# Attention and deformable-convolution block: input of the first projections loaded in blocks of 32 by 32 and transposed by VectorE

## The chip, the cores and the metric

One core of a Trainium2 chip runs the whole program; seven cores are idle. The metric is the device time of one execution in microseconds (us), lower is better.

The engines are named as in the profile: PE is TensorE's matmul stream and PEld its weight loads, DVE is VectorE, ACT is ScalarE, POOL is GpSimd, SP is SyncE. SP, ACT and POOL issue the DMAs of this kernel; SP issues nearly all.

## The reference, cut to what matters

Four images of 64 by 64 pixels with 256 channels (float32) go through two layers.

```
# layer 0, for each image b, n = 4096 tokens, CQ = 32
q, k, v   = x @ wq + bq, x @ wk + bk, x @ wv + bv     # 256 -> 32, 32, 256
x1        = gamma * softmax(q k^T) v + x
# layer 1
h         = ln(x1)
off, mask = heads(gelu(ln(depthwise3x3(h))))          # 288 offsets and 144 masks per token
s         = sum over 9 points of mask * bilinear sample of (h @ inproj)
x2        = x1 + s @ outproj
out       = x2 + fc2(gelu(fc1(ln(x2))))               # 256 -> 1024 -> 256
```

All matmuls are float32.

## The kernel before, in words

The tokens of an image are cut into 16 parts (`u`) of 256 tokens. The kernel is one software pipeline of 64 slots, one for each part of each image. In a slot PE computes the attention of one part (`e`, the energies, at L719 and `acc`, the weighted sum, at L744), and beside it the first projections of a later part, the layer-1 steps `front`, `plan` and `sample` of earlier parts, and the MLP (`back`) of a still earlier one. The projections of part u of image b+1 run in the slot of part u of image b, so slots 0 to 47 hold one projection each and slots 48 to 63 none. The projections of image 0 have no attention to run beside: they are done one after the other at the start, and `e` of slot 0 comes behind them on PE.

The change touches the function `project`, whose steps are:

- `load` (L611): one DMA of SP brings 256 tokens x 256 channels into `xs`, tokens on partitions. For image 0 `xs` lies in one of eight buffers (tag "ex"), later in a single one.
- `turn` (L619, helper at L316): four PE transposes of 128 x 128 against the identity put the part into PSUM (`pt_x`), channels on partitions. For image 0 this takes a bank of the energies, later one of two banks (tag "m") that nearly all small PE results share.
- `copy` (L622): ACT copies `pt_x` to `xT` in SBUF (three buffers).
- `keys` (L626) makes keys and queries in one PSUM tile `pkq` (two banks in turn for image 0); `key_bias` (L634) adds the biases on ACT: two `kT` pieces (L638) and `qT` (L644, two buffers), and SP writes `qT` to DRAM (`qd`, L645), from where `qs` is read for the attention.
- `values` (L647) makes `pv`; `value_bias` (L656) adds the bias on DVE into `V` for image 0 (L659), or into `vs` (L662), which SP stores for later.

The order on PE, DVE, ACT and POOL is written out by hand: every step has a time in the tables `WHEN` and `LATE`, steps are sorted by slot x 60 + that time and issued in this order, and each engine runs its instructions in order. In "project" the table has load -14.4, turn 19.72, copy 23.24, values 37.05, keys 48.45. SP's order is not written out; the framework's scheduler decides it, so an edit can move DMAs on SP.

Two more things set the order at the start. First, the DMAs of SP and ACT use eight completion counters in turn, in the order in which the scheduler placed them: a DMA is issued only when the DMA that had its counter before has landed. The small weights that ACT loads during image 0 (`loads`, L99: `gamma_s`, `g`, `b`, `inw`, ...) take their turns among SP's. Second, DVE has set-up work in the same stretch: the copies of the offset weights (`om_w`, `om_b`, L154 and L158, each behind a DMA that waits for the copy before) and the number tables (L216), which go back and forth with POOL and wait for POOL's DMAs that write zeros.

Of the kernel before, what the change touches and what calls it, by code (L numbers as in the profile page):

```python
# [8 lines left out]
F32 = mybir.dt.float32  # L9
# [7 lines left out]
def tile_attention_dcnv3_block(  # L17
# [23 lines left out]
    nc = tc.nc  # L41
    B, H, W, C = x.shape
    N = H * W
    P = 128
# [15 lines left out]
    xt_ = x.rearrange("b (t q h2) w c -> b t (h2 w) q c", q=2, h2=2)  # L60
    outs = out.rearrange("b h w c -> (b h w) c")
    out_ = outs.rearrange("(g p) c -> p g c", p=P)

    def tiles_of(v):

        return max(2 * v - 1, 0), 1 if v in (0, UN) else 2
# [9 lines left out]
    p1 = ctx.enter_context(tc.tile_pool(name="p1", bufs=1))  # L76
    main = ctx.enter_context(ExitStack())
    kv = main.enter_context(tc.tile_pool(name="kv", bufs=1))
    p8 = main.enter_context(tc.tile_pool(name="p8", bufs=8))
    win = main.enter_context(tc.tile_pool(name="win", bufs=6))  # L80
    ps_e = main.enter_context(tc.tile_pool(name="ps_e", bufs=1, space=bass.MemoryType.PSUM))
# [40 lines left out]
    for odd in range(2):  # L122
        t = const.tile([P, C // P, 4, CQ], F32, name=f"wkq{odd}")
        v = const.tile([P, 1], F32, name=f"bkq{odd}")
        for r in range(4):
            i = (r // 2 + odd) % 2
# [181 lines left out]
    def rows4(r):  # L308
        return slice(r * CQ, (r + 1) * CQ)

    def transposed(src, name, n=2, pool=None, tag="m"):

        pt = (pool or ps).tile([P, C // P, 256], F32, tag=tag, name=f"pt_{name}")
        for k in range(C // P):
            for i in range(n):
                nc.tensor.transpose(  # L316
                    pt[:, k, i * P : (i + 1) * P], src[:, i, k * P : (k + 1) * P], ident
                )
        return pt
# [283 lines left out]
    def project(b, u):  # L603


        n = f"{b}_{u}"
        first = b == 0
        odd = u % 2
        st = {}

        def load():  # L611
            if first:
                xs = p8.tile([P, 2, C], F32, tag="ex", name=f"xs_{n}")
            else:
                xs = p1.tile([P, 2, C], F32, tag="xs", name=f"xs_{n}")
            st["xs"] = xs
            nc.sync.dma_start(xs, xt_[b, u])

        def turn():  # L619
            st["pt"] = transposed(st["xs"], f"x_{n}", 2, *((ps_e, f"e{odd}") if first else ()))  # L620

        def copy():  # L622
            st["xT"] = p3.tile([P, C // P, 256], F32, tag="cT", name=f"xT_{n}")
            nc.scalar.copy(st["xT"], st["pt"])

        def keys():  # L626
            pool, tag = (ps_e, f"e{2 + odd}") if first else (ps, "m")
            st["pkq"] = pkq = pool.tile([P, 256], F32, tag=tag, name=f"pkq_{n}")
            for k in range(C // P):
                nc.tensor.matmul(  # L630
                    pkq, lhsT=wkq[odd][:, k, :], rhs=st["xT"][:, k, :], start=(k == 0), stop=(k == 1)
                )

        def key_bias():  # L634
            pkq = st["pkq"]
            for i in range(2):
                rows = rows4(2 * odd + i)
                nc.scalar.activation(  # L638
                    kTs[b % 2][u // 2][rows, :], pkq[rows, i * P : (i + 1) * P], AF.Identity,
                    bias=bkq[odd][rows, :],  # L640
                )
            rows = rows4(2 - 2 * odd)
            qT = p2.tile([P, 256], F32, tag="qT", name=f"qT_{n}")
            nc.scalar.activation(qT[rows, :], pkq[rows, :], AF.Identity, bias=bkq[odd][rows, :])  # L644
            nc.sync.dma_start(qd[b * NU + u], qT[rows, :])  # L645

        def values():  # L647
            st["pv"] = pv = ps.tile([P, 2, C], F32, tag="m", name=f"pv_{n}")
            for i in range(2):
                for k in range(C // P):  # L650
                    nc.tensor.matmul(  # L651
                        pv[:, i, :], lhsT=st["xT"][:, k, i * P : (i + 1) * P], rhs=wv_s[:, k, :],
                        start=(k == 0), stop=(k == 1),
                    )

        def value_bias():  # L656
            bias = bv_s.unsqueeze(1).to_broadcast([P, 2, C])
            if first:
                nc.vector.tensor_add(V[u][:, :, :C], st["pv"], bias)  # L659
            else:  # L660
                vs = p1.tile([P, 2, C], F32, tag="xq", name=f"vs_{n}")
                nc.vector.tensor_add(vs, st["pv"], bias)  # L662
                nc.sync.dma_start(vd[u], vs)

        return {
            "load": load, "turn": turn, "copy": copy, "keys": keys, "key_bias": key_bias,
            "values": values, "value_bias": value_bias,
        }

# [702 lines left out]
    def whole(general):  # L1372
# [10 lines left out]
        for b in range(B):  # L1383
            for u in range(NU):
                s = b * NU + u
                if b == 0:
                    put(-1, "first", project(b, u), 3.6 * u - 1.8 + WHEN["attention"]["e0"])
                else:
                    put(s - NU, "project", project(b, u))

                    i = u // 4 * 4 + u % 2 * 2
                    t = max(WHEN["attention"][f"w{j}"] for j in (i, i + 1))
                    steps.append(((NU * b - 1) * T + t + 0.5, len(steps), lambda u=u: value_load(u)))
                att = Attention(b, u, general)
                some = att.steps()
                if general and u == 0:
                    put(s, "general", {"e0": some.pop("e0"), "x0": some.pop("x0")})
                put(s, "attention", some)
                put(s, "tables", {k: lambda f=f: ready(f) for k, f in TABLES.items()})
                put(s + 1, "front", front(att))  # L1400
# [95 lines left out]
```

## Time and profile before

| | us |
|---|---|
| median of 3 runs | 3838.01 (3837.57 to 3839.95) |
| the profiled execution, its own time | 3837.92 |
| span of the profiled execution | 3835.8 |
| PE busy | 3789.8 (99%) |
| DVE busy | 3401.7 (89%) |
| ACT busy | 2199.0 (57%) |
| POOL busy | 312.9 (8%) |
| DMA queue of SP, share of 16 DMA engines | 34.5% |
| granted TensorE clock, mean | 0.997 |

An engine's busy time is the union of its instructions' spans; matmuls overlap in the pipeline, so a mean duration of one instruction is longer than what it adds to PE's stream. What an instruction adds is read from the chain of waits, which goes back from the last instruction to whatever released each piece and so counts every microsecond once. In lists of groups the numbers behind the bar are the total busy time (us), the mean of one instruction (ns), then the engine's idle time just before them (us) and what ended it. In a list of windows each row has the stretch, its length, the busy time of PE, PEld, DVE, ACT and POOL with their counts, the granted TensorE clock, the DMA engines' mean busy share and GB/s.

### The profile page before, as it was taken

How to read it: one execution, taken by the hardware profiler on the slowest of the kernel's cores; microseconds unless marked ns; L12 is line 12 of the kernel's file. 1: busy time of each engine (PE TensorE's matmuls, PEld its weight loads, DVE VectorE, ACT ScalarE, POOL GpSimd, SP SyncE). 2: the span in 40 equal slices, each digit the busy share in tenths (PEclk: the TensorE clock that was granted, in tenths of full speed). 3: DMA queues.
4: the chain of work that ended last, by engine and by line, in shares of the span. 5: the costliest groups of instructions: out<-in, count | busy, mean ns of one | idle time of the engine just before them, and what ended most of it. 6: DMA issues, size and time to landing. Idle time of an engine off the chain costs nothing.

```text
span 3835.8 us, 56185 instructions
## 1 busy us (share of the span) xinstructions
PE 3789.8 (99%) x20466; PEld 3139.2 (82%) x20466; DVE 3401.7 (89%) x6199; ACT 2199.0 (57%) x4261; POOL 312.9 (8%) x444
## 2 busy tenths in 40 slices
PE   8999999999999999999999999999999999999988
PEld 7788888888888888888888888888888888888867
DVE  2599899999998998998998999999999999999995
ACT  4556556565565565565565565655655565555543
POOL 1000000000000000000000000000000000000021
PEclk9999999999999999999999999999999999999999
DMA  5333333334343333333533333333344333333331
GB/s 151 91 102 90 96 96 93 99 90 139 97 112 92 102 92 90 106 92 90 149 99 105 97 92 99 91 95 97 100 127 112 91 86 88 98 84 84 88 93 51
DMA packets 231789, 378.03 MB, mean 99 GB/s; under 512 B 32880, under 2 KB 181936, under 8 KB 231504
## 3 DMA queue, kind: packets, MB, share of 16 engines
q1 hardware_dynamic: 221408, 367.46, 34.5%
q10 hardware_dynamic: 8512, 3.43, 0.4%
q8 instruction: 163, 2.67, 0.3%
q0 software_dynamic: 1584, 3.47, 0.3%
q14 instruction: 122, 1.00, 0.1%
HBM read 251.69 MB, written 122.56 MB: 98 GB/s over the span
## 4 chain that ended last, share of the span: by engine, by line
PE 96%; DVE 3%; DMA 1%; ACT 0%; issue 0%; SPq 0%; ACTq 0%; DVEq 0%
PE acc L744 46%; PE ph L1170 11%; PE pmlp L1187 11%; PE e L719 7%; PE po L885 5%; PE pout L1145 3%; PE pp L801 3%; PE pv L651 3%; PE pkq L630 1%; DVE pw L1064 1%; PE pt_p L316 1%; PE pc L861 1%; PE pt_f L316 1%; PE pt_s L316 1%; PE pt_b L316 1%; PE pt_x L316 1%
## 5 line engine op out<-in xcount | busy, mean ns | idle before, releaser
L744 PE MATMUL acc<-V,ex 128*128 128x257 f32 x8192 | 1900.9, 382 | 0.2
L744 PEld LDWEIGHTS acc<-V,ex 128*128 128x128 f32 x8192 | 1532.0, 190 | 264.5 <-issue 64.8
L1064 DVE TENSOR_TENSOR pw<-win,wn 128x1280 f32<-128x1280 f32 x640 | 933.8, 1486 | 9.5 <-ACT wn L1008 1.9
L1072 DVE TENSOR_TENSOR pw<-pw,pw 128x1280 f32<-128x1280 f32 x492 | 731.9, 1488 | 0.1
L732 ACT ACTIVATE ex<-e 128x512 f32<-128x512 f32 x1024 | 529.3, 602 | 63.0 <-PE e L719 54.2
L1170 PE MATMUL ph<-hT_b,f1w 128*128 128x256 f32 (+1 forms) x2080 | 493.2, 380 | 6.3 <-ACT gT L1178 2.8
L1187 PE MATMUL pmlp<-f2w,gT 128*128 128x256 f32 x2048 | 462.7, 379 | 1.3 <-DVE x1b L1152 1.1
L1170 PEld LDWEIGHTS ph<-hT_b,f1w 128*128 128x128 f32 x2080 | 381.9, 190 | 82.8 <-issue 18.9
L848 DVE SCALAR_TENSOR_TENSOR cv<-hs,dw,cv 128x256 f32<-128x256 f32 (+1 forms) x1076 | 429.9, 467 | 7.9 <-ACT cv L844 1.3
L1187 PEld LDWEIGHTS pmlp<-f2w,gT 128*128 128x128 f32 x2048 | 384.2, 190 | 51.8 <-DVE x1b L1152 1.4
L288 ACT ACTIVATE xn_p<-pc,nm_p,rstd_p 128x256 f32<-128x256 f32 x128 | 65.4, 560 | 554.1 <-DVE nm_p L280 551.2
L1178 ACT ACTIVATE gT<-ph,f1b 128x256 f32<-128x256 f32 (+1 forms) x520 | 236.5, 468 | 254.8 <-PE ph L1170 253.3
L719 PE MATMUL e<-qs,kT 32*128 32x256 f32 x4096 | 296.3, 401 | 0.7 <-ACT ex L732 0.7
L719 PEld LDWEIGHTS e<-qs,kT 32*128 32x128 f32 x4096 | 186.7, 184 | 72.3 <-issue 63.3
L732 ACT ACT_TABLE_LOAD x182 | 233.5, 1283 | 3.0
L274 POOL TENSOR_SCALAR rstd_p<-mv_p 128x2 f32<-128x2 f32 (+1 forms) x65 | 76.1, 1171 | 1703.4 <-DVE mv_p L272 1632.4
L885 PE MATMUL po<-om_w,ge 128*128 128x432 f32 x512 | 196.6, 527 | 0.7 <-ACT ge L878 0.7
L974 DVE TENSOR_TENSOR pr<-hat 128x1296 f32<-128x1296 f32 x128 | 192.7, 1505 | 0.6 <-DVE nm_b L280 0.5
L1178 ACT ACT_TABLE_LOAD x124 | 159.1, 1283 | 2.1
L878 ACT ACTIVATE ge<-pt_p,bd,gd 128x256 f32<-128x256 f32 (+1 forms) x130 | 66.0, 558 | 157.0 <-PE pt_p L316 157.0
L885 PEld LDWEIGHTS po<-om_w,ge 128*128 128x128 f32 x512 | 96.9, 190 | 71.1 <-issue 63.3
L894 DVE TENSOR_TENSOR om<-po,om_b 128x432 f32<-128x432 f32 x128 | 77.3, 605 | 87.3 <-PE po L885 87.3
(219 smaller groups left out, 3883.1 us busy)
## 6 DMA issues: line engine op xcount, KB each, us to landing
win<-xp SPq DMA_DIRECT2D x536, 320.0 KB, 4.1
omd<-om SPq DMA_DIRECT2D x63, 432.0 KB, 2.5
xs<-in_x_dram SPq DMA_DIRECT2D x64, 256.0 KB, 5.4
x<-in_x_dram SPq DMA_DIRECT2D x64, 256.0 KB, 2.7
x1d<-x SPq DMA_DIRECT2D x64, 256.0 KB, 3.2
xp<-xq SPq DMA_DIRECT2D x128, 128.0 KB, 2.4
x1b<-x1d SPq DMA_DIRECT2D x63, 256.0 KB, 2.8
spd<-sp SPq DMA_DIRECT2D x63, 256.0 KB, 2.1
```

The lines of the kernel that those rows point to most:

```text
L316: nc.tensor.transpose(pt[:, k, i * P : (i + 1) * P], src[:, i, k * P : (k + 1) * P], ident)
L719: nc.tensor.matmul(es[r][:, jj, :], lhsT=self.kT[2 * g + jj][rows4(r), :], rhs=self.qs[rows4(r), :], start=True, stop=not self.general,)
L732: nc.scalar.activation(ex, self.es[r], AF.Exp)
L744: nc.tensor.matmul(self.acc[i], lhsT=ex[:, jj, i * P : (i + 1) * P], rhs=V[t // 2][:, t % 2, :], start=(g == 0 and r == 0 and jj == 0), st ...
L848: nc.vector.scalar_tensor_tensor(dst, src, dw[:, k, j : j + 1], dst, ALU.mult, ALU.add)
L885: nc.tensor.matmul(st["po", i], lhsT=st["ge"][:, k, i * P : (i + 1) * P], rhs=om_w[:, k, :], start=(k == 0), stop=(k == 1),)
L974: nc.vector.tensor_mul(pr.rearrange("p a b c d g -> p a b (c d g)"), hat[:, :, i, 1, :].unsqueeze(1).to_broadcast([P, 3, 3, S]), hat[:, :, ...
L1064: nc.vector.tensor_mul(st[r].rearrange("p d (g c) -> p (d g) c", c=GC), src.rearrange("p d (g c) -> p (d g) c", c=GC), wns[v][:, i, r] .re ...
L1072: nc.vector.tensor_add(st[0], st[0], st[r])
L1170: nc.tensor.matmul(ph[:, :m], lhsT=f1w[:, k, c * P : (c + 1) * P], rhs=st["hT"][:, k, :m], start=(k == 0), stop=(k == 1),)
L1178: nc.scalar.activation(st["gT"][:, c, :m], st["ph", c][:, :m], AF.Gelu, bias=f1b[:, c : c + 1])
L1187: nc.tensor.matmul(po, lhsT=st["gT"][:, c, i * P : (i + 1) * P], rhs=f2w[:, c, :], start=(c == 0), stop=(c == NH - 1),)
```

## The change

`load` issues four DMAs in place of one, one for each group of 32 partitions, and reads the input in pieces of 32 channels (128 bytes). Within each block of 32 tokens by 32 channels, tokens are still on partitions, but the blocks already lie where the transposed tile needs them: `xs[32i+p, k, 32j+r]` is token 32j+p, channel 128k+32i+r. DVE's transpose then turns every 32 by 32 block in place, and writes `xT` directly from SBUF to SBUF. `turn` and its PSUM tile are gone, and the copy leaves ACT. The transpose on DVE takes the place of `copy` in the hand-written order; its time in the tables is not changed, and nothing else is.

```diff
+    xs_ = x.rearrange("b h w c -> (b h w) c")
+    def in_blocks(dst, src, t0, n):
+        dst = dst.rearrange("p k (j r) -> p k j r", r=32)
+        for i in range(P // 32):
+            nc.sync.dma_start(
+                dst[32 * i : 32 * (i + 1)],
+                bass.AP(
+                    src.tensor, src.offset + t0 * C + 32 * i, [[C, 32], [P, C // P], [32 * C, 4 * n], [1, 32]]
+                ),
+            )
...
             if first:
-                xs = p8.tile([P, 2, C], F32, tag="ex", name=f"xs_{n}")
+                xs = p8.tile([P, C // P, 256], F32, tag="ex", name=f"xs_{n}")
             else:
-                xs = p1.tile([P, 2, C], F32, tag="xs", name=f"xs_{n}")
+                xs = p1.tile([P, C // P, 256], F32, tag="xs", name=f"xs_{n}")
             st["xs"] = xs
-            nc.sync.dma_start(xs, xt_[b, u])
-
-        def turn():
-            st["pt"] = transposed(st["xs"], f"x_{n}", 2, *((ps_e, f"e{odd}") if first else ()))
+            in_blocks(xs, xs_, b * N + 256 * u, 2)
 
         def copy():
             st["xT"] = p3.tile([P, C // P, 256], F32, tag="cT", name=f"xT_{n}")
-            nc.scalar.copy(st["xT"], st["pt"])
+            nc.vector.transpose(st["xT"].rearrange("p k t -> p (k t)"), st["xs"].rearrange("p k t -> p (k t)"))
```

One part's load is 256 pieces of 1 KB before, and four DMAs of 512 pieces of 128 bytes after: 64 x 3 = 192 more DMAs on SP, 64 x 4 = 256 fewer transposes on PE, 64 fewer copies on ACT, 64 more instructions on DVE.

In the built program the order of instructions moves as follows. PE, ACT and POOL keep theirs, less what is gone. In a later slot DVE's transpose stands behind the first sum of the sampled rows (L1072), ahead of the sum with `ob` (L794). In image 0 the transposes alternate with the additions of `V` (transpose u+1 ahead of the addition for u); the transpose of part 1 stands behind the `om_b` copies, that of part 3 behind all number tables. On SP all loads of parts 0 to 9 of image 0 (40 DMAs) stand ahead of the first `qd`, and the loads of parts 10 to 15 between the following `qd`. ACT's `gamma_s` shares its counter with the third load of part 4.

More of the change, by code (lines that the diff above doesn't have):

```diff
@@ L665, in project @@
         return {
-            "load": load, "turn": turn, "copy": copy, "keys": keys, "key_bias": key_bias,
+            "load": load, "copy": copy, "keys": keys, "key_bias": key_bias,
             "values": values, "value_bias": value_bias,
```

## The prediction

> **What bounds the kernel now.** I read first the page's chain of work that ended last, by engine, then the windows over one slot in the middle, then the chain inside a slot.
>
> ```profile
> PE 96%; DVE 3%; DMA 1%; ACT 0%; issue 0%; SPq 0%; ACTq 0%; DVEq 0%
> ```
>
> Who shortens PE's stream shortens the kernel; what leaves ACT is worth nothing by itself. One whole slot, 1505.71 to 1563.92 (columns: length, then busy time of PE, PEld, DVE, ACT, POOL, granted clock, DMA share, GB/s):
>
> ```profile
> 1505.71:1563.92 58.21, 58.21 (x324) 48.37 (x316) 53.07 (x95) 34.27 (x66) 4.41 (x6) 1.00 0.34 95
> ```
>
> PE has no idle time. DVE is idle for 58.21 - 53.07 = 5.1 us, ACT for 24. The chain in the next slot shows what the removed transposes take of PE's stream: one row for all four of a part.
>
> ```profile
> 1592.85 1.73 PE ph L1170 x8
> 1594.57 0.44 PE pt_x L316 x4
> 1595.01 1.74 PE acc L744 x8
> ```
>
> Rows follow without a gap, so 0.44 us is the price on the path. (The group of these transposes gives 280 ns each; they overlap in the pipeline, so 4 x 280 would count too much.)
>
> The start is another stage. The chain there has two waits for `qd`, and only then PE's stream, with 0.44 + 0.87 + 1.73 = 3.03 us for each part of image 0:
>
> ```profile
> 19.26 6.46 DMA qd<-qT
> ...
> 26.20 2.32 DMA qd<-qT
> ...
> 41.57 0.44 PE pt_x L316 x4
> 42.01 0.87 PE pkq L630 x4
> 42.88 1.73 PE pv L651 x8
> ...
> 65.37 1.11 PE e L719 x16
> ```
>
> The first `e` at 65.37 is the mark by which I count this stage.
>
> **Steady slots: PE.** In slots 0 to 47 the four transposes go. On the chain DVE is the bound only at 144.8 to 168.8 and 195.2 to 226.7, that is in two slots. The other 46 give 46 x 0.44 = 20.2 us. In the two, PE waits for DVE anyway and DVE gets one instruction more.
>
> A rule speaks against the change: the Trainium skill, "VectorE: DVE Perf Modes", section "The three transpose paths", puts a 128 x 128 transpose on TensorE at about 390 ns and on VectorE at about 311 (bfloat16), where VectorE only turns 32 x 32 blocks, and the rules after it prefer TensorE where PSUM is a fit place for the result. By its 390 ns the 46 slots would give 46 x 4 x 0.39 = 72 us; the row's 0.44 us for four decides here.
>
> **Steady slots: DVE.** No row shows a DVE transpose. Bounds: `L154` copies 128x288 in 400 ns (a smaller tile); `L1064` handles 128x1280 with two operands in 1486 ns. The nearest row has the same tile:
>
> ```profile
> L1077 DVE TENSOR_TENSOR pw<-pw 128x512 f32<-128x512 f32 x123 | 84.2, 685 | 0.0
> ```
>
> It takes 685 ns by itself, some 0.6 back to back. I take 0.6. In the 46 slots this lies in DVE's 5.1 us of idle time; as the slot gets 0.44 shorter too, 5.1 - 1.04 = 4.1 us stay (at 1.5 us: 3.2). One of the waits that give this idle time is for `pc`:
>
> ```profile
> 1559.75 0.76 DVE L270 BATCH_NORM_STATS2 st_p<-pc 128x6 f32<-128x256 f32 x2 [1.01 <-PE pc L861]
> ```
>
> The last `cv` before it ends at 1555.2 and PE reaches `pc` at 1559.3: 4 us of cover. Without cover a slot would lose 0.6 instead of winning 0.44. In the two slots on DVE's chain I charge 2 x 0.6 = 1.2. Steady sum: -20.2 + 1.2 = -19.0 us.
>
> **Steady slots: DMA and SP.** The load becomes four DMAs. SP issues one in 0.4 to 0.5 us and is idle between those of the rows around it (1537.5 to 1539.8, 1543.3 to 1546.0). The single buffer is now released by DVE's transpose, some 3 us after PE's; behind the waiting load on SP stands the store `x1d`, which moves a few us and is read much later. The old load was issued at 1536.96 and used at 1594.57, 57 us later, so even a load several times slower is hidden. ACT's copy (0.57 us) was hidden on ACT: nothing. The PSUM tile that goes only relaxes a shared pair of banks: nothing to the worse.
>
> **Image 0: PE.** Without transposes the pace of PE is 0.87 + 1.73 = 2.60 us per part, at best 16 x 0.44 = 7 us less. But this stage hangs on DMAs, and 64 small loads replace 16.
>
> **Image 0: what a small load costs.** It has 512 pieces of 128 bytes, 32 for each of 16 DMA engines. `raw_qk` in the trace has pieces of that size (256 of them, 16 an engine). Its windows:
>
> ```profile
> 1.80:2.00 0.20, 0.00 (x0) 0.00 (x0) 0.20 (x1) 0.00 (x0) 0.00 (x0) 1.00 0.48 66
> 2.00:2.20 0.20, 0.00 (x0) 0.00 (x0) 0.20 (x1) 0.00 (x0) 0.00 (x0) 1.00 0.58 81
> 2.20:2.40 0.20, 0.00 (x0) 0.00 (x0) 0.14 (x1) 0.00 (x0) 0.00 (x0) 1.00 0.23 27
> ```
>
> Share times time is (0.48 + 0.58 + 0.23) x 0.2 = 0.26 us an engine, 16 ns a piece: a small load needs at least 32 x 16 ns = 0.51 us. By the best rate seen, 81 GB/s, its 64 KB need 0.81, and with gaps 0.87. I call this time s and take 0.7, midway; SP's issue time (0.4 to 0.5) lies below it. The far bound is that a piece costs as much as one of 1 KB does at full load, 41 ns (16 engines, about 400 GB/s): s = 1.3.
>
> The Trainium skill, "DMA: Bandwidth & Descriptors", section "Why small descriptors are slow (HBM only)", counts about 3 fixed cycles beside one for each 32 bytes: 7 cycles for 128 bytes against 35 for 1 KB. A fifth of 41 ns would be 8 ns a piece, s = 0.4 or 0.5 by issue, and the sum below would come to about 3826. Its "Specifications" ask for 512 bytes for full rate, which points the other way. No load of this form has run here.
>
> **Image 0: the queue.** On SP all 40 loads of parts 0 to 9 stand ahead of the first `qd`. `qT` has two buffers, so ACT's `qT` of part 2 waits until `qd` of part 0 has landed, and PE's keys of part 4 wait for that `qT` (two banks). Before, this cost two waits and ended at 32.66. Now, step by step:
>
> 1. DVE's transpose of part 1 stands behind the `om_b` copies (20.11 and 20.80 before, behind a 5.7 us landing among 256 KB loads). The large loads ahead of it are gone: I take 18 (14 to 21 is possible).
> 2. Keys 0.87, `kT` 0.73 and `qT` 0.47 later, ACT issues `gamma_s` at about 21.3; it lands 2.6 later (its DMA row): 23.9.
> 3. The third load of part 4 shares its counter, so SP stops there until 23.9. Then 22 loads to the end of part 9: 22 x 0.7 = 15.4, so `qd` of part 0 goes out at 39.3.
> 4. It lands behind 7 loads in flight: 7 x 0.7 + 1.5 = 6.4 (the first wait above was 6.46): 45.7. With `qT` 0.47, keys of part 4 at 46.2.
> 5. Six parts at the longer of 2.65 (PE, small gaps) and 4 s = 2.8, as loads and `qd` now alternate, then five at 2.65: 76.2. Keys and values of part 15, 2.6: `e` at 78.8, against 65.4: +13.4.
>
> The number tables on DVE (24.57 to 37.97 before, about 10 us at the least) stand ahead of the transpose of part 3 and would alone put `e` at about 69; that is the floor of this stage, +3.6.
>
> By the same steps s = 0.51 gives 72.4 (+7.0), s = 0.87 gives 88 (+22), s = 1.3 gives 110 (+45).
>
> **Sum.** The profiled execution took 3837.92 us, 0.1 below the median of 3838.01. 3837.92 - 19.0 + 13.4 = 3832.3, rounded to 3832. About 0.2% (7.7 us) is what a measurement can tell from no change, so this counts as the same (down to 3830.3), near the edge.
>
> **Rivals.**
> - *Faster: the loads flow.* If s is below some 0.65, or `gamma_s` lands before its counter matters, image 0 loses 4 to 11 us: 3837.9 - 19 + 3.6 to 11 = 3822 to 3830; at best, with nothing lost, 3819. For it: 16 ns a piece in the row, and 40 loads can be in flight without a consumer between them. Against: the 81 GB/s.
> - *Slower: a piece of 128 bytes costs what one of 1 KB does.* Then s = 1.3, image 0 is bound by its loads, and 3837.9 - 19 + 45 = 3864. This decides from s = 0.96 (30 ns a piece), where image 0 loses 27 us. For it: the low rate of `raw_qk` even when alone; against: 16 ns of busy time in the same rows.
> - *Slower: DVE becomes the bound.* If the transpose takes above 1.5 us or pushes `cv` past its 4 us of cover, the steady gain goes and image 0's loss stays: 3837.9 + 13 = 3851 or more. Against it stand 5.1 us of idle DVE in a slot.
> - *It doesn't do what it says*: out, since the order shows the transposes gone from PE.
>
> **How the numbers follow.** Forecast case (s from 0.65 to 0.96, 3830 to 3845): 0.38, its value 3832. Faster: 0.34, as the lower half of the s that the rows allow reaches it. Slower by loads: 0.20. Slower by DVE: 0.08. These are the chances of faster, same and slower: 0.34, 0.38, 0.28. The range goes from 3818, image 0 costing nothing, to 3862, near the 1 KB price.
>
> **What would show it.** Right: a slot in the middle 57.8 us long with no PE idle; DVE transposes near 0.6 us; `qd` of part 0 issued near 39 and landed near 46; the first `e` near 79. Wrong: `e` at 70 or before (loads flow), `e` past 92 with PE waiting for transposes that wait for `xs` in every part (piece price), or PE waiting for `cv` or `pw` in middle slots (DVE bound). It would also be wrong if a middle slot shrank by much more or less than 0.44 us, for then the chain row is no price.

## The result and the profile after

The changed kernel takes 3838.33 us (median of 12 runs, 3834.12 to 3840.00), the kernel before 3839.61 (12 runs, 3837.18 to 3842.84). The ratio is 0.9996, with a 95% interval of 0.9989 to 1.0004: no difference that can be measured. The prediction was 3832, no change beyond 0.2%, range 3818 to 3862.

The profiled execution took 3838.74 us, its span 3836.9, against 3837.92 and 3835.8 before. The two ends of the pipeline moved in opposite directions. First one slot in the middle, in the windows of the changed kernel (columns as before: length, PE, PEld, DVE, ACT, POOL, granted clock, DMA share, GB/s):

```profile
1500.00:1557.77 57.77, 57.77 (x314) 47.99 (x313) 53.48 (x96) 33.81 (x65) 4.41 (x6) 1.00 0.36 96
```

The same step now recurs after 57.77 us, where it took 58.21: the 0.44 us of the removed transposes have become time. PE still has no idle time. DVE is idle for 57.77 - 53.48 = 4.3 us (5.1 before). The groups of the changed kernel have the new instruction, and the timeline of DVE shows the wait for `pc`, which has become shorter:

```profile
L636 DVE STREAM_TRANSPOSE xT<-xs 128x512 f32<-128x512 f32 x64 | 45.1, 704 | 4.4 <-DMA xs<-in_x_dram 4.4
```

```profile
1511.63 0.76 DVE L285 BATCH_NORM_STATS2 st_p<-pc 128x6 f32<-128x256 f32 x2 [0.30 <-PE pc L873]
```

A transpose takes 704 ns by itself, 0.63 back to back (222.46 to the next start at 223.09). DVE now waits 0.30 us for `pc`, where it waited 1.01.

At the other end is image 0. The timeline of PE there (start, duration, instruction, and in brackets the idle time before it and what ended it; rows between are left out):

```profile
20.90 2.07 PE L642 MATMUL pkq<-xT,wkq 128*128 128x256 f32 x4 [2.09 <-DVE xT L636]
...
32.30 2.05 PE L642 MATMUL pkq<-xT,wkq 128*128 128x256 f32 x4 [4.30 <-DVE xT L636]
34.14 3.62 PE L663 MATMUL pv<-wv_s,xT 128*128 128x256 f32 x8
43.08 2.07 PE L642 MATMUL pkq<-xT,wkq 128*128 128x256 f32 x4 [5.32 <-ACT qT L656]
...
54.99 1.13 PE L642 MATMUL pkq<-xT,wkq 128*128 128x256 f32 x4 [1.38 <-ACT qT L656]
...
58.51 1.13 PE L642 MATMUL pkq<-xT,wkq 128*128 128x256 f32 x4 [0.66 <-ACT qT L656]
...
81.29 1.15 PE L731 MATMUL e<-qs,kT 32*128 32x256 f32 x16
```

The first `e` starts at 81.29. The same view of the kernel before has it at 65.30, so 16.0 us are lost here:

```profile
65.30 1.15 PE L719 MATMUL e<-qs,kT 32*128 32x256 f32 x16
```

The keys of parts 4 and 7 to 10 (43.08, 54.99, 58.51 and two left out) wait for `qT`, and `qT` for a landed `qd`. What SP did meanwhile, in its timeline (start, duration, instruction):

```profile
12.82 27.68 SPq L72 DMA_DIRECT2D xs<-in_x_dram  x36
40.60 0.56 SPq L657 DMA_DIRECT2D qd<-qT  x1
41.27 2.60 SPq L72 DMA_DIRECT2D xs<-in_x_dram  x4
43.97 0.56 SPq L657 DMA_DIRECT2D qd<-qT  x1
44.63 2.60 SPq L72 DMA_DIRECT2D xs<-in_x_dram  x4
```

Apart from one stop of 2.0 us for `gamma_s` (its row stands under run 7) and shorter ones, SP issued small loads back to back, and each issue took 0.63 us in median (in the view of the tile, minimum, median and maximum in ns):

```profile
L72 SPq DMA_DIRECT2D xs<-in_x_dram x22: 578/630/639, 25.8 to 39.9; - x22
```

The account by the marks of the two traces closes. The marks behind the first `e` are two blocks of 32 `acc` matmuls, 44 slots apart, in the chain of waits; before:

```profile
241.84 6.93 PE acc L744 x32
2803.22 6.93 PE acc L744 x32
```

and after:

```profile
261.60 6.93 PE acc L756 x32
2803.66 6.93 PE acc L756 x32
```

First `e`: +16.0. From there to the first mark, which ends slot 3: +3.8. Then the 44 slots: 2561.38 us before, 2542.06 after, -19.3. The rest: +0.7. Sum +1.1, the difference of the spans.

### The profile page after: what moved, and what is told of

It reads as the page before. It is cut to its first block, busy times and chain, and to the rows that moved or that the text cites. A ratio compares the mean times of both kernels' runs of the same rounds, so it can differ in the third digit from the quotient of the medians.

```text
span 3836.9 us, 56054 instructions
## 1 busy us (share of the span) xinstructions
PE 3771.2 (98%) x20210; PEld 3120.2 (81%) x20210; DVE 3432.8 (89%) x6263; ACT 2167.7 (56%) x4197; POOL 313.2 (8%) x444
## 4 chain that ended last, share of the span: by engine, by line
PE 92%; DVE 3%; issue 0%; ACT 0%; DMA 0%; SPq 0%; DVEq 0%; ACTq 0%
PE acc L756 45%; PE ph L1182 11%; PE pmlp L1199 11%; PE e L731 7%; PE po L897 5%; PE pout L1157 3%; PE pp L813 3%; PE pv L663 2%; PE pkq L642 1%; PE pt_s L331 1%; PE pt_p L331 1%; PE pc L873 1%; PE pt_b L331 1%; PE pt_f L331 1%; DVE pw L1076 1%; DVE cv L860 1%
```

## The experiments

All runs of a comparison share one chip with runs of the kernel before. "First e" is from PE's timeline.

**1. Images 1 to 3 alone.** The step functions keep the old form where `by_pe` holds:

```diff
+        by_pe = first
...
+            if by_pe:
+                nc.sync.dma_start(xs, xt_[b, u])
+            else:
+                in_blocks(xs, xs_, b * N + 256 * u, 2)
```

(`turn` and `copy` likewise.)

> Image 0 keeps the PE transposes and large loads; only images 1 to 3 (slots 0 to 47) get block loads and the DVE transpose. Theory (steady gain and first-image loss are separate and cancel): first e back at 65.4 us, slots in the middle 57.77 us long against 58.21, so 44 slots x 0.44 = 19.4 us less, given back 1 to 3 us in slots 2 and 3, where DVE is the bound: 16 to 19 us faster than before. Rival (the middle slots' gain is given back elsewhere, later, or there is no loss in image 0): within 4 us of the time before.

Measured 3820.57 us against 3838.60, ratio 0.9952 (0.9939 to 0.9966): 18.0 us faster. First e at 63.36; a slot in the middle 57.77.

The mark of the first e is not as sharp as its decimals. Runs 1, 3 and 4 leave the code of image 0 as it was before, and yet their first e starts at 63.36, 64.79 and 63.62, against 65.30 (in runs 1 and 4 SP issues small loads of image 1 among those of image 0). A move of up to some 2 us in this mark is no evidence by itself.

**2. Image 0 alone.**

```diff
+        by_pe = not first
```

> Only image 0 gets block loads and the DVE transpose; images 1 to 3 keep the old form. Theory: first e near 81.3 us as in the whole change, slots 58.21 us as before, so 14 to 18 us slower than before. Rival (image 0's late start is absorbed in the pipeline, or the loss belongs to later slots): within 4 us of the time before.

Measured 3856.43 us, ratio 1.0044 (1.0030 to 1.0057): 17.8 us slower. First e at 80.53, slots of 58.21. The two halves add up to -0.2 us; the whole change has -1.3. Gain and loss are separate, and each is about as large as the traces said.

**3. Images 1 to 3 without the first four parts.**

```diff
+        by_pe = first or (b == 1 and u < 4)
```

> As the run that changes images 1 to 3 only, but the first four parts of image 1 (slots 0 to 3, where DVE is the bound) also keep PE transposes. Theory: 44 slots x 0.44 = 19.4 us less and nothing given back in slots 2 and 3: 18 to 20 us faster than before, 0 to 3 us better than with those four changed. Rival (slots 2 and 3 don't care): the same as with those four changed, or 0.9 us worse since slots 0 and 1 lose their 0.44.

Measured 3818.66 us, ratio 0.9948 (0.9934 to 0.9961), the lowest median of all kernels here, some 20 us below before. It isn't told apart from run 1 by the times. The traces do tell slots 0 to 3 apart: from the first `e` to the `acc` mark of slot 4 (241.43 and 240.87) run 1 needs 178.07 us and this one 176.08, so the four DVE transposes there cost 2.0 us net, and in run 1 a lower clock, described below, takes 1.7 us in slot 3; the mark of the first `e` lies 1.4 later here, which takes most of that away.

**4. How much cover DVE has.** In run 1, three transposes too many for each part:

```diff
             else:
+                for _ in range(3):
+                    nc.vector.transpose(st["xT"].rearrange("p k t -> p (k t)"), st["xs"].rearrange("p k t -> p (k t)"))
                 nc.vector.transpose(st["xT"].rearrange("p k t -> p (k t)"), st["xs"].rearrange("p k t -> p (k t)"))
```

> As the run that changes images 1 to 3 only, but every part is transposed four times on DVE (three transposes too many, 3 x 0.63 = 1.9 us of DVE in each slot; the output is not touched by it). Theory (DVE has 5.1 us of idle time a slot, 4 us of cover ahead of pc): middle slots stay at 57.77 us; only slots 2 and 3 pay 2 x 1.9 us, so 3 to 7 us slower than that run. Rival (DVE is as good as bound): 44 x 1.9 = 83 us slower. Between them, a cover of only 1 us: some 40 us slower.

```profile
1500.00:1557.77 57.77, 57.77 (x320) 48.05 (x312) 55.43 (x100) 33.79 (x65) 4.40 (x7) 1.00 0.36 95
```

That is a middle slot of this kernel: DVE is busier by 1.95 us and the slot is as long as in run 1. The total, 3823.03 us (ratio 0.9960, 0.9946 to 0.9974), is 2.5 above run 1, a little below the 3 to 7 expected. So in the middle slots 2.6 us of transposing would have been hidden too; the DVE rival never was near.

**5. Piece size.** Image 0 with as many DMAs and bytes, in pieces of 1 KB:

```diff
-            in_blocks(xs, xs_, b * N + 256 * u, 2)
+            if first:
+                for i in range(4):
+                    nc.sync.dma_start(xs[32 * i : 32 * (i + 1)], xt_[b, u][32 * i : 32 * (i + 1)])
+            else:
+                in_blocks(xs, xs_, b * N + 256 * u, 2)
```

> As the whole change, but image 0's four DMAs of a part read 32 tokens x 2 x 256 channels each: the same 64 KB to the same 32 partitions in pieces of 1 KB, 64 in place of 512 (tokens stay in the old order, so the transposed values are not the reference's). Theory A (the 0.63 us that SP needs to issue a small load grows with its pieces and sets the pace): issue falls below 0.5 us, qd of part 0 goes out near 32 in place of 40.6, first e near 72. Theory B (SP pays per DMA, whatever is in it): issue stays at 0.63, first e at 81. Theory C (the DMA engines' time for pieces sets the pace): issue as in B while they wait, but landings get shorter and first e lies between.

```profile
L634 SPq DMA_DIRECT2D xs<-in_x_dram x34: 311/426/1029, 13.7 to 32.3; - x34
```

The issue on SP fell from 630 to 426 ns, the first `qd` went out at 32.79, and the first `e` starts at 67.87, 4 us earlier than expected (3824.06 us in all, ratio 0.9959, 0.9945 to 0.9974). Theory A holds: SP's time for one issue depends on what the DMA contains, 64 pieces of 1 KB or 512 of 128 bytes, and sets the pace. 13.4 of the 16.0 us hang on this. Since the bytes were kept, the number of pieces and their size changed together; which of the two the issue time follows is not shown.

**6. Two queues.**

```diff
-            nc.sync.dma_start(
+            (nc.scalar if split and i % 2 else nc.sync).dma_start(
```

(with `split` on for image 0)

> As the whole change, but image 0's small loads are issued by SP and ACT in turn. Theory A or B (SP's issue sets the pace): twice the rate, DMA share in the windows up from 0.62 towards 1, all loads of parts 0 to 9 issued by about 28, first e between 68 and 75. Theory C (pieces set the pace, 98 GB/s): the rate stays, first e near 80.

Measured 3834.26 us, ratio 0.9988 (0.9978 to 0.9998), first e at 78.19: a miss for the numbers of A and B. Windows of this kernel, and one of the whole change, show why it is not a clean answer:

```profile
24.00:28.00 4.00, 0.24 (x2) 0.00 (x0) 2.23 (x5) 0.00 (x0) 0.99 (x3) 1.00 1.13 161
28.00:32.00 4.00, 0.00 (x0) 0.00 (x0) 0.43 (x2) 0.04 (x1) 1.68 (x5) 0.59 0.96 125
```

```profile
28.00:32.00 4.00, 0.00 (x0) 0.00 (x0) 1.67 (x7) 0.00 (x0) 1.24 (x6) 0.89 0.62 97
```

With one queue the DMA engines were busy 62% of the time at 97 GB/s; with two they reach 96 to 113%, at 125 to 161 GB/s. So SP did set the pace, but the pieces are a second limit close behind. And SP's issue got no longer beside full DMA engines, so it is not a wait for them:

```profile
L72 SPq DMA_DIRECT2D xs<-in_x_dram x19: 578/579/730, 13.3 to 33.2; - x19
```

Besides, ACT did nothing else while it issued its loads: its first `kT` ran at 33.26, against 16.65 in the whole change. SP in turn waited 8.2 us in all for counters that loads held and 5.3 for buffers that the transposes had not yet freed. How much each cost is open.

**7. The wait for qd.** Two parts share a `qT` tile in image 0, on different partitions:

```diff
+            if not first or not odd:
+                pairs[0] = p2.tile([P, 256], F32, tag="qT", name=f"qT_{n}")
+            qT = pairs[0]
-            qT = p2.tile([P, 256], F32, tag="qT", name=f"qT_{n}")
```

> As the whole change, but in image 0 two parts share one qT tile (even parts on partitions 64 to 95, odd on 0 to 31), so the two buffers hold four parts, and qT of part 4, not of part 2, waits for qd. Loads and their order on SP are the same up to qd of part 0. Theory (PE waits for qd of part 0 behind 40 loads, by way of two qT buffers): PE goes on with parts 4 and 5, waits before part 6 near 46 us, first e at 74 to 77. Rival (loads or the number tables hold PE by themselves): first e stays at 80 to 81.

Measured 3839.91 us, ratio 1.0004 (0.9994 to 1.0013), first e at 82.25: a miss. Parts 4 and 5 did go ahead (keys at 37.36 and 40.01), but `qd` of part 0 went out at 45.72, not 40.6. The list of SP's waits (in all, times, longest):

```profile
SPq L72 <- DMA b<-in_L_conv_ln_b_dram: 5.1, 1, 5.1
SPq L72 <- DMA gamma_s<-in_L_conv_gamma_dram: 2.0, 1, 2.0
```

A load had the completion counter of the small weight `b`, which ACT issues only behind the keys of part 3. The coupling that the prediction named for `gamma_s` struck at another place.

**8. The same without that coupling.** The small weights go to slot 0:

```diff
-            steps += [(3.5 * i - 55.0, len(steps) + i, fn) for i, fn in enumerate(loads)]
+            steps += [(2.9 * i + 1.0, len(steps) + i, fn) for i, fn in enumerate(loads)]
```

> As the run with two parts in one qT tile (where SP waited 5.1 us for the counter of the small weight b, which ACT loads behind the keys of part 3, so that qd of part 0 went out at 45.7), and ACT's small weights are loaded in slot 0, after the first e, so no load on SP can wait for them. Theory (shared counters moved the wait): SP issues the 40 loads without a stop, qd of part 0 goes out at 38 to 39, keys of part 6 near 45, first e at 74 to 76. Rival (the stop was something else, or PE is held by the loads' pace): first e at 80 to 83 as in that run.

Measured 3833.86 us, ratio 0.9986 (0.9977 to 0.9996). `qd` of part 0 at 39.38, keys of part 6 at 45.33, first e at 76.46. Each as expected, within half a microsecond: counters had taken the gain of run 7.

**9. qd from ACT's queue.**

```diff
-            nc.sync.dma_start(qd[b * NU + u], qT[rows, :])
+            (nc.scalar if first else nc.sync).dma_start(qd[b * NU + u], qT[rows, :])
```

> As the whole change, but image 0's qd stores are issued by ACT, right behind the qT that they write, so no qd stands behind the small loads on SP; the loads themselves keep their number, pieces and queue. Theory (the first qd behind 40 loads, and the later ones between loads, are what holds PE): qd of part 0 goes out near 18 in place of 40.6, PE is held only by the number tables (transpose of part 3 near 31) and then by loads, which SP issues at 0.65 us each, 2.6 us a part: first e at 67 to 71, total 10 to 14 us less than the whole change. Rival (the loads' own pace holds PE, wherever qd stands): first e at 78 or later.

Measured 3846.05 us, ratio 1.0015 (1.0005 to 1.0025), first e at 82.75: slower, and a miss. `qd` of part 0 went out at 17.58, but now SP's loads stood still for ACT's DMAs, 21.6 us for the six longest of these waits. Three of them:

```profile
SPq L72 <- DMA b<-in_L_conv_ln_b_dram: 5.4, 1, 5.4
SPq L72 <- DMA qd<-qT: 4.7, 2, 2.7
SPq L72 <- DMA dw<-in_L_conv_dw_w_dram: 3.6, 1, 3.6
```

**10. The same with the small weights in slot 0** (the edit of run 8).

> As the run in which ACT issues image 0's qd (where SP's loads waited 21.6 us in all for counters that DMAs of ACT held: b 5.4, qd 4.7, dw 3.6, gamma_s 3.1, f1w 2.7, ow 2.1), and ACT's small weights are loaded in slot 0, after the first e. Theory (a load on SP takes 0.65 us of issue; what else held image 0 was qd standing behind loads, and shared counters): SP issues 64 loads in 45 us with stops of at most 5 us, for qd counters and buffers; PE is held by the number tables up to 32, then goes at 2.6 to 3 us a part: first e at 66 to 71, total 10 to 15 us less than the whole change less what the weights cost in slot 0 (1 to 2 us). Rival (the loads' pace alone holds image 0): first e at 76 or later.

Measured 3834.53 us, ratio 0.9988 (0.9979 to 0.9998), first e at 73.86: 7.4 us earlier than in the whole change, but 3 to 8 later than expected. SP still waited 12.7 us in all for the counters of `qd`; the keys go at about 3.1 us a part and wait for `xT`. So some 7 of the 16 us go with `qd` behind loads and the small weights' counters together; no run moves the weights alone, and the rest, the loads' own pace and counters, I can't divide further. The total is only 3.8 us below the whole change's 3838.33. One reason is in the trace: at 92.73, in slot 0, PE waits 3.62 us for ACT's `ex`, after ACT itself had waited 6.6 us for a `win` load of SP. `ex` does not read `win`, so this looks like a shared counter again; that is not shown further.

**11. The clock.** Spare matmuls in PE's waits of image 0:

```diff
+            if first and u in (3, 4):
+                spare = ps_e.tile([P, 256], F32, tag=f"e{odd}", name=f"spare_{n}")
+                for _ in range(14):
+                    nc.tensor.matmul(spare, lhsT=ident, rhs=wv_s[:, 0, :], start=True, stop=True)
```

> As the whole change, with 14 spare matmuls (128x256, into an unused bank) ahead of the keys of parts 3 and 4, in PE's waits of 4.3 and 5.3 us. Theory (after a wait of some us PE gets half its clock; keys and values of parts 3 and 4 ran at a granted clock of 0.50, and 4 took 5.2 us in place of 2.6): clock 1.00 from 43 us on, first e 2 to 3 us earlier, at 78 to 79.5. Rival (the clock there is off the path, since SP paces parts 5 to 9): first e stays at 81 or comes later.

Measured 3836.97 us, ratio 0.9996 (0.9987 to 1.0006), first e at 81.61. The granted clock was 1.00 from 28 us on, and the keys of part 5 came at 47.12 in place of 48.27, but those of part 7 at 55.45, no earlier than 54.99. The rival holds: from part 5 on SP's 3.36 us a part set the time, and the half clock ahead of it lay beside that.

## Why the prediction was right, and where it was off

**Steady slots: right.** Predicted 46 slots x 0.44, 44 of them in this stretch, 19.4 us; measured 19.32 us there, 0.439 each. The row of the chain was the price. The transpose was put at 0.6 and is 0.63 in sequence; 4.1 us of DVE idle time were to stay and 4.3 did.

**Slots 0 to 3: mis-sized.** The prediction has +0.3 us for them (-0.88 in two, +1.2 in two); the traces +3.8. Most of the missing part is the granted clock, which the prediction didn't weigh. In slot 3 PE waits for DVE's `x1b` in both kernels, 1.32 us before and 2.61 after, with another transpose ahead of it on DVE:

```profile
226.81 1.10 PE L630 MATMUL pkq<-xT,wkq 128*128 128x256 f32 x4 [1.32 <-DVE x1b L1193]
245.10 1.10 PE L642 MATMUL pkq<-xT,wkq 128*128 128x256 f32 x4 [2.61 <-DVE x1b L1205]
```

Behind the longer wait the clock is halved. Windows of the changed kernel:

```profile
240.00:242.50 2.50, 2.50 (x20) 1.60 (x12) 2.50 (x4) 0.00 (x0) 0.00 (x0) 1.00 0.00 0
242.50:245.10 2.60, 0.00 (x0) 0.03 (x1) 2.60 (x7) 0.00 (x0) 1.60 (x2) 1.00 0.57 150
...
246.00:247.00 1.00, 1.00 (x4) 0.79 (x4) 1.00 (x3) 0.47 (x2) 0.00 (x0) 0.57 0.81 159
247.00:248.00 1.00, 1.00 (x3) 0.80 (x3) 1.00 (x2) 0.55 (x2) 0.00 (x0) 0.50 0.96 247
```

The eight `acc` matmuls at 246.04 took 3.53 us, those of before (227.75) 1.90: 1.6 us lost to the clock beside 1.3 of wait. All kernels with the DVE transpose in slot 3, ten of them, have this wait (2.60 or 2.61), and in nine the `acc` matmuls behind it are slowed (2.74 to 3.55 us for eight); run 3, without that transpose, has neither. But run 4 has the wait and no dip: its clock stays at 1.00 there. So the longer wait comes with the transpose, and the dip nearly always with the wait; what decides in the tenth is open. In slot 0 the clock was 0.71 between 84 and 88 us, where before the same stretch (68 to 72) had 1.00, and 1.7 us were lost. The wait just before it, 0.67 us, is the same in both kernels; what lowers the clock there is open.

The Trainium skill, "TensorE: Matmul & The Clock Gate", section "Part 1: The HAM clock gate", says that the clock falls to one half after at least one idle window of about 3.4 us. Here shorter ones were enough: 2.6 us in slot 3, and 2.09 in image 0, where the keys at 20.90 ran at 0.50. A wait of 3.63 us in run 9, on the other hand, left the clock at 1.00. The two waits without a dip, of run 4 and run 9:

```profile
230.74 1.10 PE L656 MATMUL pkq<-xT,wkq 128*128 128x256 f32 x4 [2.61 <-DVE x1b L1219]
48.67 1.10 PE L642 MATMUL pkq<-xT,wkq 128*128 128x256 f32 x4 [3.63 <-DVE xT L636]
```

Four such matmuls take 1.10 us here and 2.07 at half clock (20.90 above). So by these traces the length of the last wait alone does not decide; the measurement stands over the page's figure.

**Image 0: right in the path, wrong in what prices a load, 2.6 us short in the sum.** The path was `qd` behind 40 small loads, then `qT`, then the keys. Step by step, predicted and measured:

| step | predicted | measured |
|---|---|---|
| transpose of part 1 | 18 | 20.14 |
| `gamma_s` issued | 21.3 | 23.02 |
| time of a small load, s | 0.7 | 0.65 |
| `qd` of part 0 issued | 39.3 | 40.60 |
| `qT` of part 2, after it landed | 45.7 | 42.56 |
| keys of part 4 | 46.2 | 43.08 |
| a part while loads and `qd` alternate | 2.8 | 3.4 to 4.1 (parts 7 to 10) |
| six parts, from the keys of part 4 to those of part 10 | 16.8 | 22.5 |
| first e | 78.8 | 81.29 |

Two terms were wrong and partly cancelled. `qd` was to wait 6.4 us behind 7 loads in the DMA engines; it landed in less than 2, at a DMA share of 0.62, so the keys of part 4 came 3.1 us early. The six parts behind them then took 5.7 us more than the sum had. The prediction's step was 4 s = 2.8; SP's own row has four issues (2.60), one `qd` (0.56) and gaps, 3.36 us at the least: the issue of `qd` had been left out.

The price of a load was close for the wrong reason. It was worked out from the DMA engines (16 ns a piece, 81 GB/s), with "SP's issue time (0.4 to 0.5) lies below it"; but SP's issue itself grew to 0.63 us, as run 5 shows, and s = 0.65 is that issue. The first step was off in its cause too: the transpose of part 1 did not wait for the `om_b` copies, done by 17.6, but for its own loads:

```profile
20.14 0.71 DVE L636 STREAM_TRANSPOSE xT<-xs 128x512 f32<-128x512 f32 x1 [2.58 <-DMA xs<-in_x_dram]
```

**The sum.** The misses of image 0 (2.6 us), of slots 0 to 3 (3.5) and of the rest (0.7) point the same way and make up the 6.7 us between the forecast's -5.6 (3832.3 against 3837.92) and the +1.1 of the spans. That the two sides nearly cancel was foreseen; that they cancel to about 1 us was not, and is an accident of these sizes.

**The rivals.** Loads that flow (s below 0.65) missed by little: s was 0.65, and run 5 shows about the time that this rival would have had. A piece as dear as one of 1 KB is out: a window with a share of 0.62 and 0.65 us for 32 pieces gives 12.6 ns a piece, not 41. DVE as the bound is out by run 4.

## What to carry to other kernels

A price read off the chain of waits, per slot and per instruction, held here where the engine is full, even for a gain of 0.44 us; but this pipeline's first stage has no such cover, and the same edit cost about as much there as all later slots gave, so it is worth making the edit only where it pays. When one DMA is split into many with small pieces, count them at the issuing engine, with its issue time measured for that form, and look at what is queued behind them there. DMAs that share completion counters couple queues that look independent: taking one wait away can bring in another at the next counter.

## What the runs showed of the hardware

- The issue of a DMA on SP took 0.43 us with 64 pieces of 1 KB (run 5) and 0.63 with 512 pieces of 128 bytes in the whole change (medians); in run 6, with two queues and the DMA engines at about full share, the latter took 0.58 on SP and 0.59 on ACT.
- 128-byte pieces into 32 partitions: 97 GB/s from one queue at a DMA share of 0.62, 125 to 161 GB/s from two at about full share.
- PE's granted clock fell to 0.50 for some 3 us after waits of 2.09 and 2.6 us in the whole change, and stayed at 1.00 after one of 1.3 before, one of 2.61 in run 4 and one of 3.63 in run 9; spare matmuls in the waits kept it at 1.00 in run 11.
